# Moving the making of weight forms from GpSimd to VectorE, and reordering two pairs of steps in the tail, in a fused two-layer graph network

## The chip, the cores and the metric

The kernel runs on one NeuronCore of a Trainium2 chip, with all data in float32. The metric is the device time of one execution in microseconds (us), the median of three runs. Engines are named as the profile names them: PE is TensorE (PEld its weight loads), DVE is VectorE, ACT is ScalarE, POOL is GpSimd, and SP is SyncE, which issues most of the DMA transfers.

## The reference

There are 128 graphs of 128 nodes with 256 features, x of shape (128, 128, 256), and a 0/1 adjacency matrix for each. Two layers follow one another. Cut to what matters:

```
# layer 0: attention with 8 heads, values by relation, then a feed-forward part
q, k = x @ Wq + bq, x @ Wk + bk
attn = softmax(q k^T / sqrt(32))
out  = sum over r of (attn * (adj == r)) @ (x @ Wv[r] + bv[r])
x    = norm(x + out @ Wo + bo)
x    = norm(x + gelu(x @ W1 + b1) @ W2 + b2)          # W1 256x1024, W2 1024x256
# layer 1: two graph-attention layers, then a feed-forward part
for W, a in ((W1g, a1), (W2g, a2)):
    h   = h @ W
    att = softmax over axis 1 of where(adj > 0, leaky_relu(h a_l + (h a_r)^T), -9e15)
    h   = att @ h
x = norm(x + h)
x = norm(x + relu(x @ w_ff1 + b_ff1) @ w_ff2 + b_ff2)
```

## The kernel before

The tokens are worked on in 32 groups of four graphs (512 tokens). A group passes through these stages: projections to q, k and v; attention; first feed-forward part (first_ffn); two graph layers (layer1); second feed-forward part (second_ffn). Several groups are in flight at once, each in another stage.

The large products (projections, both feed-forward parts) are done with seven block products in place of eight, a Winograd form of Strassen's scheme. For this each weight is held as four blocks, B11, B21, B22 and one more, and needs four more forms, T1 to T4, that are differences of blocks. The function combined(w), lines 182 to 184, makes them once for each weight, by four subtractions: T3 = B22 - T1 (the slot T1 holds the fourth block at first), T1 = T1 - B11, T2 = B22 - T1, T4 = B21 - T2. For w1, w2, u1 and u2 (the two feed-forward parts' weights) each subtraction covers 128x512 elements, for wqk and wv 128x256. The two groups at the start use the plain blocks of wqk and wv, so T1 of these may only be overwritten when those projections are done (the generator projections; the later one is projected).

The order of the work is written out by hand. Each stage is a Python generator that gives out one unit of work at a time; in_order(...) calls them in the order of its arguments, and a pair (f1, 4) means four units of f1. A callable in the list, such as lambda: combined(w1), is issued at that place. Each engine takes its own instructions strictly in that order; PE, ACT, DVE, SP and POOL all run this way. The names in the lists: pr and pr1 are projections, at and at1 attention, n0, n1_ and so on the steps of a norm, f1 and f2 the units of the two feed-forward parts, gwu the making of the graph layers' weights, l1 the units of layer1, turned the transposition of a group ahead of a feed-forward part.

Lines that the steps below name:

- L184: the four subtractions of combined.
- L725, masked: the exponentials e are multiplied by adj, four times 128x512, to give pm. L754, sums: the products pav of e and pm with v. L771, L773 and L776 divide by the sums.
- L595: the second half of v gets its bias, read from PSUM; L594 is ACT's copy of the first half.
- L334, L335, L344, L349: the norm's variance plus eps (DVE), its power -1/2 (POOL), the shift (DVE), and the scaling of x by ACT. L367: the multiplication and the addition of the norm's rows.
- In ffn, one pass r over half of the hidden columns issues the units in this order: T3 (into the bank called pe, copied to p7 by L456), T2 (into seeded, copied to p16 by L460), B21 (into pa, activated by L435), T1 (into seeded; L466 adds p7, then L435), T4 (into pe; L470 adds p16, then L435), the next pass's B11, and B22 (into seeded; L435, then L479 to L481 make h2 and h3, then L483 seeds the bank again). There are two passes; product2 (L420) follows.
- In layer1: pw (L862) are the products with the graph weights, one for each of the four graphs, evicted by ACT's copies wh (L866). pr (L815) spreads a column, L834 adds it, L838, L840 and L844 to L851 make the attention matrix gs. py (L875) are the products with gs, evicted by ACT's copies yh (L878). The products pg (L888) end the second graph layer. pw and py each use banks of the pool ps_s, of which there are two, so that the third product waits until the first has been evicted.

Only the last group, in the tail after the loop, has layer1 interleaved with the second feed-forward part of the group ahead of it and with nothing else.

Of the kernel before, what the change touches and what calls it, by code (L numbers as in the profile page):

```python
# [107 lines left out]
def fast_pass(ctx, tc, a, out):  # L108
# [5 lines left out]
    nc = tc.nc  # L114
# [22 lines left out]
    def load_xT(g):  # L137

        xt = (w2p if g == 1 else w1p).tile(
            [P, NCH, T], F32, tag="yT" if g == 1 else "xT", name=f"xT_{g}"  # L140
        )
        nc.sync.dma_start(
            xt, xT[:, g * T : (g + 1) * T].rearrange("(c p) t -> p c t", p=P)
        )
        return xt
# [20 lines left out]
    def halved(name, half):  # L166


        kh, nh = half(0).shape[0] // 2, half(0).shape[1]
        w = k.tile([P, 7, kh // P, nh], "w_" + name)  # L170

        for i, j, h in ((B11, 0, 0), (B21, 1, 0), (T1, 0, 1), (B22, 1, 1)):
            nc.sync.dma_start(
                w[:, i], half(h)[j * kh : (j + 1) * kh, :].rearrange("(c p) n -> p c n", p=P)
            )
        return w

    def forms(name):
        nh = a[name].shape[1] // 2
        return halved(name, lambda h: a[name][:, h * nh : (h + 1) * nh])  # L180

    def combined(w):
        for o, p, q in ((T3, B22, T1), (T1, T1, B11), (T2, B22, T1), (T4, B21, T2)):
            nc.gpsimd.tensor_sub(w[:, o], w[:, p], w[:, q])  # L184


    temp = flat(w1p.tile([P, NF, T], F32, tag="hT", name="temp"))
# [10 lines left out]
    first = dict(g=0, direct=0, xt=load_xT(0))  # L198
    wqk = halved("qk", lambda h: a["L0_gnn_W" + "qk"[h]])
# [3 lines left out]
    wv = halved("v", lambda h: a["L0_gnn_Wv"][h])  # L203
# [14 lines left out]
    w1, b1 = forms("L0_gnn_W1"), k.col("L0_gnn_b1")  # L218
# [4 lines left out]
    w2 = forms("L0_gnn_W2")  # L223
# [13 lines left out]
    u1, c1 = forms("L1_gnn_w_ff1"), k.col("L1_gnn_b_ff1")  # L237
    u2 = forms("L1_gnn_w_ff2")
# [55 lines left out]
    def transposed(y, gc, bc, n):  # L294

        yT = w2p.tile([P, NCH, T], F32, tag="yT", name="yT_" + n)
        for c in range(NCH):
            pt = ps_s.tile([P, T], F32, tag="s", name=f"pt_{n}_{c}")
            for b in range(G):
                nc.tensor.transpose(  # L300
                    pt[:, b * P : (b + 1) * P], y[:, b, c * P : (c + 1) * P], k.ident
                )
            nc.scalar.activation(  # L303
                yT[:, c, :], pt, AF.Identity, bias=bc[:, c : c + 1], scale=gc[:, c : c + 1]
            )
        return yT
# [74 lines left out]
    def turned(S, i):  # L381
        n = f"{i}_{S['g']}"
        S["xT", i + 1] = yT = transposed(S["x"], *cols[i], n)
        if i == 1:
            return

        S["yS", i + 1] = ys = w1p.tile([P, 4, TH], F32, tag="yS", name="yS_" + n)
        a11, a21, a12, a22 = (yT[:, c, h * TH : (h + 1) * TH] for c in range(2) for h in range(2))
        nc.vector.tensor_sub(ys[:, 2], a11, a21)
        nc.vector.tensor_add(ys[:, 0], a21, a22)  # L390
        nc.vector.tensor_sub(ys[:, 1], a22, ys[:, 2])
        nc.vector.tensor_sub(ys[:, 3], a12, ys[:, 1])
# [142 lines left out]
    def table(func):  # L535

        nc.scalar.activation(k.none, k.eps[:1], func)

    gelu, exp = lambda: table(AF.Gelu), lambda: table(AF.Exp)
# [384 lines left out]
    with tc.manual_schedule(engines={ET.PE, ET.Activation, ET.DVE, ET.SP, ET.Pool}):  # L924


        for _ in range(4):
            nc.tensor.matmul(seeded, k.ident, over(k.ident), start=True, stop=True)
        none = iter(())
        st = [first, second] + [None] * (NG - 2)  # L930
        S1 = st[1]
        gwu, pr, at = graph_weights(), projections(first), attention(first)
        pr1, at1 = projections(S1), attention(S1)
        n0, n1_, n0_ = norm(first, 0), norm(first, 1), norm(S1, 0)

        def output_bias():
            pb = mm_tile("pb0")
            for c in range(NCH):
                nc.tensor.matmul(
                    pb[:, :D], b0[:, c : c + 1].to_broadcast([P, P]), wo[:, c, :],  # L940
                    start=(c == 0), stop=(c == NCH - 1),
                )
            nc.vector.tensor_add(bo, bo, pb[:, :D])
            prepared(first)

        in_order(
            lambda: combined(w1), (pr, 4), (at, 2), (pr, 2), at, (pr, 2), at, lambda: combined(w2), (at, 3), (pr1, 2),
            at, output_bias, at, (pr1, 2), (at, 3), pr1, at, (at1, 2), n0, n0, pr1, at1, lambda: turned(first, 0), (at1, 2),
        )
        f1 = first_ffn(first)  # L950
        prepared(S1)
        st[2] = entered(2)
        pr = projected(st[2])
        in_order(
            gelu, (f1, 4), pr1, f1, f1, at1, at1, f1, pr1, lambda: combined(wqk), lambda: combined(wv), lambda: combined(u1), f1, n0, at1, (f1, 2), n0, f1, at1,
            (f1, 3), gwu, at1, f1, gwu, f1, at1, gwu,
            f1, at1, f1, gwu, at1, lambda: combined(u2), f1, n0_, pr, n0_, (f1, 4), n1_, (pr, 5), lambda: turned(S1, 0),
        )
        for g in range(NG - 1):
            S, S1 = st[g], st[g + 1]  # L960
            more = g + 2 < NG
            f1, f2 = first_ffn(S1), second_ffn(S)
            n1, n2 = norm(S1, 1), norm(S, 2)
            at = n0 = none
            if more:
                S2 = st[g + 2]
                at, n0 = attention(S2), norm(S2, 0)
            ahead = lambda: turned(S, 2)
            ready = (lambda: prepared(st[g + 2])) if more else (lambda: None)
            if g == 0:  # L970
                l1 = layer1(S)
                in_order(
                    f1, n1_, (pr, 2), (f1, 3), lambda: turned(S, 1), (pr, 2), f1, (n0_, 2), f1, l1, f1, (n1_, 2), l1, l1, f1, l1,
                    (f1, 2), (l1, 2), (pr, 2), f1, l1, (pr, 2), f1, pr, l1, f1, l1, f1, (l1, 2), exp, f1, (at, 2), (l1, 2),
                )
            else:
                n3 = norm(st[g - 1], 3)
                in_order(
                    pr, lambda: turned(S1, 0), (pr, 2), *(() if more else (f2_,)), f1, l1, gelu, (pr, 2), f2_, n3, f1, l1, pr,
                    n0_, f1, (pr, 2), (f1, 3), n0_, l1, f1, (pr, 2), l1, f1, n3, (pr, 2), f1, l1, f1, n3, (pr, 2),  # L980
                    (f1, 3), n3, lambda: store(st[g - 1]), f1, (n1_, 2), exp, (at, 2), f1, (l1, 3),
                )
            in_order(
                f1, (pr, 2), l1, f1, (pr, 2), at, f1, (pr, 2), l1, n2, (pr, 2), f1, n2, (pr, 2), f1, (pr, 2), f1, (pr, 2), *((ahead,) if more else ()), at, f1, n1,
                *(() if more else (ahead,)),
            )
            if not more:
                break
            l1 = layer1(S1)
            pr = none  # L990
            if g + 3 < NG:
                st[g + 3] = entered(g + 3)
                pr = projected(st[g + 3])
            in_order(
                f2, at, (f2, 2), n1, at, f2, at, (f2, 2), lambda: turned(S1, 1), f2, at, (n2, 2), (f2, 2),
                at, f2, l1, ready, (f2, 3), l1, f2, at, f2, l1, (f2, 2), at, at, f2, at, n0, l1, f2,
                n0, l1, pr, f2, *((f2,) if g + 3 < NG else ()),
            )
            n0_, n1_, f2_ = n0, n1, f2
        in_order(f2, n1, (f2, 2), lambda: turned(S1, 1))  # L1000
        l1 = layer1(S1)
        in_order(
            (f2, 2), (l1, 3), f2, l1, (f2, 2), (l1, 2), n1, (f2, 2), l1, n1, (f2, 2), (l1, 2), f2, l1, n2, f2, (l1, 3), n2,
            (f2, 3), l1, (f2, 2), l1,
        )
        n2, n3 = norm(S1, 2), norm(S, 3)
        in_order(n2, f2, n2, (f2, 3), lambda: turned(S1, 2))
        f2 = second_ffn(S1)
        in_order(f2, n3, (f2, 3), n2, n3, (f2, 4), n2, n3, (f2, 4), n3, lambda: store(S), (f2, 2))
        checks()  # L1010
        in_order((f2, 6))
        root(S1, 3, pair(1))
        in_order(f2)
        normed(S1, 3, pair(1))
        in_order(f2)
        root(S1, 3, pair(0))
        for p in (1, 0):
            if p == 0:
                normed(S1, 3, pair(0))
            for step in range(2):  # L1020
                scaled(S1, 3, step, (p,))
            store(S1, pair(p))
# [345 lines left out]
```

## Time and profile before

Time: 2780.09 us, median of 3 runs (2779.88 to 2780.28). The profiled execution has a span of 2778.7 us and a mean granted PE clock of 0.996.

| engine | busy, us | share of the span | instructions |
|---|---|---|---|
| PE | 2725.9 | 98% | 21621 |
| PEld | 2372.0 | 85% | 21621 |
| DVE | 2287.3 | 82% | 5296 |
| ACT | 1613.9 | 58% | 3589 |
| POOL | 166.7 | 6% | 161 |

Matmuls are pipelined, and their ends are modelled, so that a busy PE isn't PE at its peak. Of POOL's 166.7 us, 133.4 us are the 129 powers of L335, spread over the whole run, and 30.9 us the 24 subtractions of L184, all in the first 87 us. In the lines of a group the columns after the bar are the busy time and the mean duration of one in ns, and after the second bar the idle time of the engine just ahead of these instructions, with what ended it. In a timeline a line is: start in us, duration in us, engine, source line, operation, out<-in, shape, count, and in brackets the idle time before and what ended it; several like instructions are merged, so the start of the next line can lie within a merged one.

### The profile page before, as it was taken

Reading aid. Unit: us, or ns where it says so; the run is one execution under the profiler, and the core shown is the slowest. Engines: PE = TensorE matmul, PEld = TensorE weight load, DVE = VectorE, ACT = ScalarE, POOL = GpSimd, SP = SyncE. Lnnn points to the kernel's source line nnn. Section 1 sums busy time; section 2 is a strip of 40 time slices with the busy share of each in tenths; the row PEclk is TensorE's granted clock in tenths of the full one; section 3 lists DMA queues with packets and bytes.
Section 4 is the critical chain, followed back from the end, with each engine's and each line's share of the span. In section 5 each row is a group of like instructions: output and inputs, shape, how many; then the busy total and the mean of one; then the engine's idle time right before and its main releaser. Section 6 shows DMA issues by size and latency. Waiting matters only on the chain.

```text
span 2778.7 us, 54158 instructions
## 1 busy us (share of the span) xinstructions
PE 2725.9 (98%) x21621; PEld 2372.0 (85%) x21621; DVE 2287.3 (82%) x5296; ACT 1613.9 (58%) x3589; POOL 166.7 (6%) x161
## 2 busy tenths in 40 slices
PE   8899999999999999999999999999999999999997
PEld 5688888888888888888888888888888888888876
DVE  5778888888888888888888888888888888888876
ACT  4456556556565566565565565565655665655653
POOL 2200000000000000000000000000000000000000
PEclk9999999999999999999999999999999999999999
DMA  6001100010100101000101000111001110001000
GB/s 177 1 24 32 35 16 28 32 35 32 35 16 24 35 32 35 24 28 24 35 32 35 16 30 29 35 31 35 17 24 35 32 35 27 25 24 35 13 12 17
DMA packets 70234, 86.12 MB, mean 31 GB/s; under 512 B 8428, under 2 KB 48728, under 8 KB 69976
## 3 DMA queue, kind: packets, MB, share of 16 engines
q1 hardware_dynamic: 68872, 82.20, 9.5%
q8 instruction: 172, 2.82, 0.4%
q14 instruction: 86, 0.70, 0.1%
q10 hardware_dynamic: 1104, 0.40, 0.1%
HBM read 65.68 MB, written 16.90 MB: 30 GB/s over the span
## 4 chain that ended last, share of the span: by engine, by line
PE 89%; ACT 4%; DVE 3%; issue 3%; DMA 1%; SPq 0%; ACTq 0%; POOL 0%; DVEq 0%; POOLq 0%
PE po L420 16%; PE ph L411 13%; PE seeded L411 13%; PE seeded L420 12%; PE pqqa L641 4%; PE pwo L789 4%; PE pw L862 4%; PE pvqa L641 4%; PE pav L754 3%; PE pt L300 3%; PE pvqb L641 3%; PE pqqb L641 3%; PE ps L709 2%; PE py L875 2%; PE pg L888 2%
## 5 line engine op out<-in xcount | busy, mean ns | idle before, releaser
L349 ACT ACTIVATE x<-x,sh,rs 128x256 f32<-128x256 f32 x388 | 201.4, 590 | 424.3 <-DVE sh L344 424.3
L335 POOL TENSOR_TENSOR rs<-rs,mhalf 128x4 f32<-128x4 f32 x129 | 133.4, 1034 | 2554.3 <-DVE rs L334 2310.6
L466 DVE TENSOR_TENSOR hT<-seeded,p 128x512 f32<-128x512 f32 x128 | 88.5, 691 | 156.0 <-ACT hT L435 89.5
L411 PE MATMUL seeded<-yS,w_L_gnn_w_ff 128*128 128x256 f32 x768 | 207.3, 392 | 4.9 <-ACT seeded L483 2.2
L411 PE MATMUL seeded<-yS,w_L_gnn_W 128*128 128x256 f32 x768 | 202.0, 386 | 3.2 <-ACT seeded L483 2.2
L411 PE MATMUL ph<-yT,w_L_gnn_w_ff 128*128 128x256 f32 x768 | 200.9, 385 | 0.9 <-ACT yT L303 0.9
L411 PE MATMUL ph<-yT,w_L_gnn_W 128*128 128x256 f32 x768 | 197.4, 379 | 0.4 <-ACT yT L303 0.4
L320 DVE BATCH_NORM_STATS2 st<-x 128x6 f32<-128x256 f32 x512 | 192.1, 417 | 6.7
L411 PEld LDWEIGHTS seeded<-yS,w_L_gnn_w_ff 128*128 128x128 f32 x768 | 138.1, 190 | 63.1 <-ACT seeded L483 28.1
L420 PE MATMUL po<-w_L_gnn_W,hT 128*128 128x128 f32 x1536 | 190.0, 277 | 0.0
L420 PEld LDWEIGHTS po<-w_L_gnn_W,hT 128*128 128x128 f32 x1536 | 183.9, 192 | 6.8
L420 PE MATMUL po<-w_L_gnn_w_ff,hT 128*128 128x128 f32 x1536 | 187.0, 275 | 0.0
L420 PEld LDWEIGHTS po<-w_L_gnn_w_ff,hT 128*128 128x128 f32 x1536 | 184.1, 192 | 3.3
L411 PEld LDWEIGHTS ph<-yT,w_L_gnn_w_ff 128*128 128x128 f32 x768 | 141.1, 190 | 43.3 <-issue 25.2
L411 PEld LDWEIGHTS seeded<-yS,w_L_gnn_W 128*128 128x128 f32 x768 | 138.5, 190 | 40.6 <-DVE hT L466 12.1
L725 DVE TENSOR_TENSOR pm<-e,adj 128x512 f32<-128x512 f32 x256 | 170.2, 725 | 0.0
L411 PEld LDWEIGHTS ph<-yT,w_L_gnn_W 128*128 128x128 f32 x768 | 145.6, 190 | 20.8 <-ACT yT L303 0.7
L435 ACT ACTIVATE hT<-hT,c_L_gnn_b 128x256 f32<-128x256 f32 x256 | 109.5, 497 | 60.2 <-DVE hT L466 58.5
L715 ACT ACTIVATE e<-ps 128x512 f32<-128x512 f32 x256 | 129.8, 589 | 7.5 <-PE ps L709 7.4
L435 ACT ACTIVATE hT<-hT,c_L_gnn_b_ff 128x256 f32<-128x256 f32 x256 | 110.1, 514 | 33.9 <-DVE hT L466 29.6
L834 ACT ACTIVATE gs<-spread,wh 128x128 f32<-128x128 f32 x120 | 38.4, 390 | 156.9 <-DMA spread<-hbm 156.9
L420 PEld LDWEIGHTS seeded<-w_L_gnn_W,hT 128*128 128x128 f32 x1024 | 124.3, 192 | 3.5 <-DVE hT L517 0.2
(196 smaller groups left out, 6522.0 us busy)
## 6 DMA issues: line engine op xcount, KB each, us to landing
xT<-in_xT_dram SPq DMA_DIRECT2D x32, 512.0 KB, 5.8
x<-in_x_dram SPq DMA_DIRECT2D x32, 512.0 KB, 5.1
out_dram<-x SPq DMA_DIRECT2D x31, 512.0 KB, 2.9
spread<-hbm SPq DMA_DIRECT2D x59, 256.0 KB, 3.2
adj<-in_adjT_dram SPq DMA_DIRECT2D x32, 256.0 KB, 4.2
w_L_gnn_W<-in_L_gnn_W_dram SPq DMA_DIRECT2D x8, 256.0 KB, 6.7
w_L_gnn_w_ff<-in_L_gnn_w_ff_dram SPq DMA_DIRECT2D x8, 256.0 KB, 5.0
hbm<-line SPq DMA_DIRECT2D x59, 2.0 KB
```

Source lines behind the costliest of these rows:

```text
L320: nc.vector.bn_stats(st[:, b % 2, :], S["x"][:, b, :])
L335: nc.gpsimd.tensor_tensor(rs[:, bs], rs[:, bs], k.mhalf[:, bs], op=ALU.pow)
L349: nc.scalar.activation(x[:, b, :], x[:, b, :], AF.Identity, bias=sh[:, b : b + 1], scale=rs[:, b : b + 1],)
L411: nc.tensor.matmul(bank[:, s * TH : (s + 1) * TH], wa[:, form, 0, f * P : (f + 1) * P], m, start=start and s == 0, stop=True, skip_group_c ...
L420: nc.tensor.matmul(bank[:, s * P : (s + 1) * P], m[:, f, s * P : (s + 1) * P], wb_[:, form, f, :], start=start and s + f == 0, stop=True, ...
L435: nc.scalar.activation(o[:, s], o[:, s] if src is None else src[:, s * TH : (s + 1) * TH], func, bias=ba[:, f : f + 1],)
L466: nc.vector.tensor_add(hidden(1, 1, r), halves(seeded), halves(p7))
L641: nc.tensor.matmul(bank[:, s * TH : (s + 1) * TH], *ops, start=start and s == 0, stop=True, skip_group_check=True,)
L715: nc.scalar.activation(e[:, s], pss[s], AF.Exp, scale=SCALE)
L725: nc.vector.tensor_mul(pm[:, s], S["e", p][:, s], S["ad"][:, pair(p), None, :].to_broadcast([P, 2, NCH, P]),)
L789: nc.tensor.matmul(po[:, s * D : (s + 1) * D], oT[:, c, b * P : (b + 1) * P], wo[:, c, :], start=(c == 0), stop=(c == NCH - 1),)
L862: nc.tensor.matmul(pw[:, :NU], yT[:, c, b * P : (b + 1) * P], wu[:, c, :], start=(c == 0), stop=(c == NCH - 1),)
```

## The change

GpSimd no longer makes the forms; the same 24 subtractions are issued on VectorE, each moved in the written order to a place meant to meet an idle VectorE: w1 not at the start but after the second step of the first norm; w2 in the first feed-forward part of the first group, after four of its units; wqk and wv somewhat earlier and apart; u1 and u2 at the start of the first turn of the main loop. In the tail, one feed-forward unit (T1 of either pass) is put between the first and the second pair of pw and of py, where before both pairs followed after it.

```
     def combined(w):
         for o, p, q in ((T3, B22, T1), (T1, T1, B11), (T2, B22, T1), (T4, B21, T2)):
-            nc.gpsimd.tensor_sub(w[:, o], w[:, p], w[:, q])
+            nc.vector.tensor_sub(w[:, o], w[:, p], w[:, q])
...
         in_order(
-            lambda: combined(w1), (pr, 4), (at, 2), (pr, 2), at, (pr, 2), at, lambda: combined(w2), (at, 3), (pr1, 2),
-            at, output_bias, at, (pr1, 2), (at, 3), pr1, at, (at1, 2), n0, n0, pr1, at1, lambda: turned(first, 0), (at1, 2),
+            (pr, 4), (at, 2), (pr, 2), at, (pr, 2), (at, 4), (pr1, 2),
+            at, output_bias, at, (pr1, 2), (at, 3), pr1, at, (at1, 2), n0, n0, lambda: combined(w1), pr1, at1, lambda: turned(first, 0), (at1, 2),
         )
...
         in_order(
-            gelu, (f1, 4), pr1, f1, f1, at1, at1, f1, pr1, lambda: combined(wqk), lambda: combined(wv), lambda: combined(u1), f1, n0, at1, (f1, 2), n0, f1, at1,
+            gelu, (f1, 4), lambda: combined(w2), pr1, f1, f1, at1, at1, f1, lambda: combined(wqk), pr1, lambda: combined(wv), f1, n0, at1, (f1, 2), n0, f1, at1,
             (f1, 3), gwu, at1, f1, gwu, f1, at1, gwu,
-            f1, at1, f1, gwu, at1, lambda: combined(u2), f1, n0_, pr, n0_, (f1, 4), n1_, (pr, 5), lambda: turned(S1, 0),
+            f1, at1, f1, gwu, at1, f1, n0_, pr, n0_, (f1, 4), n1_, (pr, 5), lambda: turned(S1, 0),
         )
...
             if g == 0:
                 l1 = layer1(S)
                 in_order(
-                    f1, n1_, (pr, 2), (f1, 3), lambda: turned(S, 1), (pr, 2), f1, (n0_, 2), f1, l1, f1, (n1_, 2), l1, l1, f1, l1,
+                    f1, n1_, lambda: combined(u1), lambda: combined(u2), (pr, 2), (f1, 3), lambda: turned(S, 1), (pr, 2), f1, (n0_, 2), f1, l1, f1, (n1_, 2), l1, l1, f1, l1,
...
         in_order(f2, n1, (f2, 2), lambda: turned(S1, 1))
         l1 = layer1(S1)
         in_order(
-            (f2, 2), (l1, 3), f2, l1, (f2, 2), (l1, 2), n1, (f2, 2), l1, n1, (f2, 2), (l1, 2), f2, l1, n2, f2, (l1, 3), n2,
+            f2, l1, f2, (l1, 2), f2, l1, (f2, 2), (l1, 2), n1, (f2, 2), l1, n1, f2, l1, f2, l1, f2, l1, n2, f2, (l1, 3), n2,
             (f2, 3), l1, (f2, 2), l1,
         )
```

## The prediction

> **What bounds the kernel now.** I read the page's share of each engine first: PE is busy for 98% of the span, so a change can only win where PE is held up. The 40 slices show that this is at the two ends (8 in the first slice, 7 in the last, 9 between). So I then read the waits of PE in the first 160 us, the busy times by stretch, and the timeline of both ends.
>
> The largest wait of PE there (columns: total us, times, longest), and the stretch 78 to 93 us (busy us of PE, PEld, DVE, ACT and POOL, the granted clock, the DMA):
> ```profile
> PE pav L754 <- DVE pm L725: 7.8, 8, 3.3
> 78.00:93.00 15.00, 8.90 (x70) 6.10 (x71) 11.61 (x9) 2.13 (x7) 8.77 (x6) 0.66 0.00 0
> ```
> PE waits for VectorE's masking (pm), at 0.66 of its clock, while GpSimd works. The timeline of that place, and the same masking in a later group:
> ```profile
> 73.66 13.43 POOL L184 TENSOR_TENSOR w_L_gnn_w_ff<-w_L_gnn_w_ff 128x512 f32<-128x512 f32 x8
> 75.84 3.43 DVE L367 TENSOR_TENSOR x<-x,r_L_gnn_g 128x512 f32<-128x512 f32 x2
> 79.19 6.76 DVE L725 TENSOR_TENSOR pm<-e,adj 128x512 f32<-128x512 f32 x4
> 89.13 1.85 PE L411 MATMUL seeded<-yS,w_L_gnn_W 128*128 128x256 f32 x4
> ...
> 2625.10 2.48 DVE L725 TENSOR_TENSOR pm<-e,adj 128x512 f32<-128x512 f32 x4
> ```
> Four masks take 6.76 us beside GpSimd and 2.48 us alone; four 128x256 products take 1.85 us there against 1.03 elsewhere. GpSimd's work that the change removes (mean ns of one ahead of the bar's end):
> ```profile
> L184 POOL TENSOR_TENSOR w_L_gnn_w_ff<-w_L_gnn_w_ff 128x512 f32<-128x512 f32 x8 | 13.0, 1624 | 0.5
> L184 POOL TENSOR_TENSOR w_L_gnn_W<-w_L_gnn_W 128x512 f32<-128x512 f32 x8 | 11.8, 1476 | 22.2 <-DMA w_L_gnn_W<-in_L_gnn_W_dram 21.7
> L184 POOL TENSOR_TENSOR w_v<-w_v 128x256 f32<-128x256 f32 x4 | 3.2, 807 | 16.8 <-PE pv L590 16.6
> L184 POOL TENSOR_TENSOR w_qk<-w_qk 128x256 f32<-128x256 f32 x4 | 2.9, 726 | 0.2
> ```
>
> [...]only such instructions stretch (L725, L367, L479 to L481), from about 0.6 us to 1.1 to 1.75 us each; reciprocals beside heavy DMA keep their 1.7 us, and two L555 adds at 37.3 us, with the DMA engines full and GpSimd idle, take their usual 1.29 us. [...]a pair of one GpSimd and one VectorE instruction takes 1.67 us here, about what GpSimd's takes. [...]here 1.48 to 1.62 us against 0.69. [...]Here PE has nearly nothing from 77.7 us, and the matmuls are at half speed from 81 us on.
>
> **The change, part one: the head.** Prices from the trace: independent 128x512 adds on VectorE start every 0.605 us (L367), dependent ones every 0.71 us (L479 to L480); for 128x256 it is 0.34 and 0.46 us (L389 to L392). In the built program each of a weight's last three subtractions waits for the one before it, so one combined() costs 3x0.71 + 0.61 = 2.74 us, or 3x0.46 + 0.34 = 1.72 us for wqk and wv. In all 4x2.74 + 2x1.72 = 14.4 us of new VectorE work. Where it goes are four idle times of VectorE (in brackets, what ended them):
> ```profile
> 53.70 0.42 DVE L595 TENSOR_TENSOR v<-pv,bv 128x256 f32<-128x256 f32 x1 [2.40 <-ACT v L594]
> 64.41 0.42 DVE L595 TENSOR_TENSOR v<-pv,bv 128x256 f32<-128x256 f32 x1 [2.79 <-ACT v L594]
> 71.76 0.42 DVE L595 TENSOR_TENSOR v<-pv,bv 128x256 f32<-128x256 f32 x1 [3.07 <-ACT v L594]
> 124.93 0.69 DVE L466 TENSOR_TENSOR hT<-seeded,p 128x512 f32<-128x512 f32 x1 [5.36 <-PE seeded L411]
> ```
> w1 goes ahead of the first (2.40 us, and 0.5 more because L344, 0.68 us beside GpSimd, is 0.15 alone), w2 ahead of the second, wqk ahead of the third, u1 and u2 ahead of the fourth. 2.74 in 2.9, 2.74 in 2.79 and 1.72 in 3.07 cost nothing; 5.48 in 5.36 costs 0.1 us. Only wv, behind the third L595, has work queued behind it that PE waits for (L479 to L481, L367, pm): 1.72 us on the path. All these weights have long landed, as GpSimd read w1 at 18.6 and w2 at 30.1 us.
>
> What is won, along the path:
> 1. First attention: from the first pav product to the next scores 3.70 us (24.27 to 27.97), for what takes 1.77 us undisturbed (2614.60 to 2616.37). 1.9 us.
> 2. Second attention: from the first pav to the next projection 2.58 us (36.16 to 38.74) against 1.77. 0.8 us, together 2.7; a further 0.1 at the third. The second xT, issued at 17.0 us and landing in at most 7.3 us, doesn't hold this up.
> 3. From VectorE's L479 (72.10) to the end of the four masks (85.95): 13.85 us. Without GpSimd: 1.72 for wv, 0.71 + 2x0.61 for L479 to L481, 2x0.605 for L367, 3x0.605 + 0.69 for the masks, 7.36 us. 6.5 us, together 9.3.
> 4. The clock, if it stays up: the remaining pav products take 1.72 us instead of 3.13 (86.00 to 89.13), and those from 89.13 to 91.83 take 1.77 instead of 2.70. 2.3 us.
> Sum: 2.8 + 6.5 + 2.3 - 0.1 = 11.5 us. From 92 us on the order is unchanged and each engine follows the others, so I carry it to the end undiminished. The loads for the third group are issued at 42 to 45 us and don't come into it.
>
> **Part two: the tail.** The two moved pairs of rows on PE (py_0, py_1 and pw_0, pw_1) go ahead of a unit called T1 here, whose product goes into seeded. Now:
> ```profile
> 2712.48 0.69 DVE L851 TENSOR_TENSOR gs<-gs,gr 128x512 f32<-128x512 f32 x1
> 2713.23 1.14 PE L875 MATMUL py<-wh,gs 128*128 128x258 f32 x4 [0.44 <-DVE gs L851]
> 2714.29 0.68 DVE L466 TENSOR_TENSOR hT<-seeded,p 128x512 f32<-128x512 f32 x1
> 2715.01 0.91 ACT L435 ACTIVATE hT<-hT,c_L_gnn_b_ff 128x256 f32<-128x256 f32 x2 [2.41 <-DVE hT L466]
> 2715.82 0.62 ACT L878 COPY yh<-py 128x258 f32<-128x258 f32 x2
> 2716.22 1.14 PE L875 MATMUL py<-wh,gs 128*128 128x258 f32 x4 [1.86 <-ACT yh L878]
> ```
> The copy of py_0 stands behind T1's activation, that behind L466, that behind L367 (2713.09), and PE behind the copy, for a bank. In the new order T1's product (0.87 us) no longer fills the wait for L851, so PE is idle about 1.6 us ahead of py_0; but then py_0/1, T1, py_2/3 follow without a gap. From the end of unit B21 to the start of T4: now 2711.56 to 2717.20, 5.64 us; then 1.66 + 3x0.87 = 4.27 us. 1.4 us. For pw the second half of yT isn't evicted before 2699.50, so pw_0 can't use all of its earlier place: the last pw ends at 2703.43 for 2703.6, and pr 0.3 us sooner. Together 1.7 us; what follows (pr, gs, pg, the norms) is one chain and moves along.
>
> 2780.1 - 11.5 - 1.7 = **2766.9 us**.
>
> **The rivals.** (a) PE loses its clock even so: it has sparse work from 74.9 to 76.6 us (new times), and after a gap of 1.81 us in the tail (2736.42) products at 2739 us ran at 1.85 us. Then the 2.3 us stay: 2769.2. Against: the gap is shorter than that of before, and dense work comes just ahead. (b) The tail's swap gives nothing, as PE idles for L851 in place of the bank: 2768.6. Against: the sum above; for: such reckoning of a few tenths over four engines is loose. (c) The gain of the head is swallowed later, by something that doesn't move along, a load or a wait I have not seen: 2780.1 - 1.7 to 2780.1 - 6, about 2776. Against: PE at 98% with small waits. (d) Slower: the 14.4 us of subtractions all come to lie on VectorE's path, as the slots are tight, and what is won is only the 7.8 us that PE is seen waiting for pm: 2780.1 + 14.4 - 7.8 = 2786.7. Against: the four idle times are measured, and as long as what goes in, to 0.1 us.
>
> **Chances.** Forecast 0.72, (a) 0.12, (b) 0.08, (c) 0.04, (d) 0.04. The forecast's own looseness is about 1.5 us either way (a combined() between 4x0.605 and 4x0.71, the pipelining of PE); with (a) and (b) inside, the range is 2764.5 to 2770.5. Faster by over 0.2% (5.6 us) are the first three: 0.92; (c) 0.04 the same; (d) 0.04 slower.
>
> **What would show it.** In the new profile: no L184 on POOL; L184 on DVE at 0.69 and about 0.4 us; L725 at 0.69 us everywhere; the unit now at 91.83 us begun near 80.3; PEclk at 1.00 in 70 to 90 us; L466 (now 124.93) idle about zero before; py_2 without a wait and py_0 with one of about 1.6 us. I am wrong if L725 stays long without GpSimd, if L595 now waits behind L184, or if the start of the main loop moves by over 2 us less than the head's sum.

## The result, and the profile after

| | before | after |
|---|---|---|
| median of 4 runs each, us | 2779.99 (2779.53 to 2780.28) | 2769.52 (2769.24 to 2769.79) |
| span of the profiled execution, us | 2778.7 | 2767.9 |
| mean granted clock of PE | 0.996 | 0.998 |
| POOL busy, us (instructions) | 166.7 (161) | 136.0 (137) |

The ratio of the times is 0.9962, 95% interval 0.9945 to 0.998. The change makes the kernel 10.5 us faster; 13.2 us had been forecast, and 2769.5 us lies within the range that was given.

The stretch from 78 to 93 us, in the columns of the prediction (busy us of PE, PEld, DVE, ACT and POOL, the granted clock, the DMA):

```profile
78.00:93.00 15.00, 15.00 (x146) 13.80 (x138) 11.84 (x29) 3.43 (x9) 0.00 (x0) 1.00 0.00 1
```

and PE's wait for the masks in the list of waits of the first 160 us:

```profile
PE pav L754 <- DVE pm L725: 0.8, 4, 0.2
```

In this stretch PE is busy throughout at full clock, where it was busy for 8.90 us at 0.66 of it, and of 7.8 us of waiting 0.8 are left. VectorE's timeline shows where the subtractions L184 went (start, duration, and in brackets the idle time before):

```profile
49.26 2.87 DVE L184 TENSOR_TENSOR w_L_gnn_W<-w_L_gnn_W 128x512 f32<-128x512 f32 x4
52.20 0.42 DVE L595 TENSOR_TENSOR v<-pv,bv 128x256 f32<-128x256 f32 x1
...
70.04 0.42 DVE L595 TENSOR_TENSOR v<-pv,bv 128x256 f32<-128x256 f32 x1 [1.36 <-ACT v L594]
70.38 1.79 DVE L184 TENSOR_TENSOR w_v<-w_v 128x256 f32<-128x256 f32 x4
...
75.22 2.49 DVE L725 TENSOR_TENSOR pm<-e,adj 128x512 f32<-128x512 f32 x4
...
109.05 5.64 DVE L184 TENSOR_TENSOR w_L_gnn_w_ff<-w_L_gnn_w_ff 128x512 f32<-128x512 f32 x8
114.61 0.69 DVE L466 TENSOR_TENSOR hT<-seeded,p 128x512 f32<-128x512 f32 x1
```

The first of the three L595 now follows w1's forms without idle time, u1 and u2 fill the place ahead of L466 (begun at 124.93 us before), and the last four masks of the second group take 2.49 us for 6.76.

The tail on PE, where py had waited 0.44 and 1.86 us. First the two pr (L815) of the kernel before, which had no wait ahead of them:

```profile
2703.67 1.12 PE L815 MATMUL pr<-ident,wh 128*128 128x128 f32 x8
...
2718.06 1.05 PE L815 MATMUL pr<-ident,yh 128*128 128x128 f32 x8
```

and the changed kernel, with two lines of ScalarE:

```profile
2693.71 1.16 PE L815 MATMUL pr<-ident,wh 128*128 128x128 f32 x8 [0.30 <-ACT wh L866]
...
2703.30 1.14 PE L875 MATMUL py<-wh,gs 128*128 128x258 f32 x4 [1.50 <-DVE gs L851]
2704.28 1.03 PE L411 MATMUL seeded<-yS,w_L_gnn_w_ff 128*128 128x256 f32 x4
2705.14 1.03 PE L875 MATMUL py<-wh,gs 128*128 128x258 f32 x4
...
2706.14 0.91 ACT L435 ACTIVATE hT<-hT,c_L_gnn_b_ff 128x256 f32<-128x256 f32 x2 [1.29 <-DVE hT L466]
2706.95 0.62 ACT L878 COPY yh<-py 128x258 f32<-128x258 f32 x2
2707.35 1.16 PE L815 MATMUL pr<-ident,yh 128*128 128x128 f32 x8 [0.32 <-ACT yh L878]
```

py behaves as forecast: 1.50 us ahead of the first pair and nothing ahead of the second. But pr, the next in the chain, now waits 0.30 and 0.32 us for ScalarE's copies, which stand behind the activation L435 and with it behind VectorE's L466.

For the comparison of all runs two stretches serve, both between events on PE. The **head** goes from the first projection pq to the first pgt (L264, behind the second group's attention), the **tail** from the last po (L420) ahead of the last group's feed-forward work to the first pt (L300) of the last norm.

| kernel | first pq | head, us | tail, us | median time, us |
|---|---|---|---|---|
| before | 6.83 | 89.54 | 49.24 | 2779.99 |
| after | 7.87 | 78.07 | 48.91 | 2769.52 |
| after again (e5) | 7.68 | 78.07 | 48.91 | 2770.44 |
| head alone (e1) | 7.70 | 78.07 | 50.83 | 2771.62 |
| head alone again (e12) | 7.15 | 79.78 | 49.23 | 2771.59 |
| head alone, PE filled (e6) | 7.93 | 78.07 | 49.79 | 2770.66 |
| tail alone (e2) | 7.58 | 87.92 | 48.91 | 2779.12 |
| wv later (e3) | 6.52 | 77.63 | 48.91 | 2767.87 |
| swap of py alone (e4) | 6.61 | 78.07 | 48.47 | 2769.26 |
| GpSimd reads beside it (e7) | 6.63 | 86.76 | 48.93 | 2779.79 |
| GpSimd only writes (e8) | 7.74 | 78.07 | 48.93 | 2769.92 |
| last copies on VectorE (e9) | 7.11 | 79.77 | 47.96 | 2769.09 |
| all three improvements (e10) | 6.41 | 77.61 | 47.46 | 2766.26 |
| before, PE filled (e11) | 7.69 | 87.26 | 49.24 | 2778.32 |

In the first comparison the times of each kernel lay within 0.8 us; in the later ones those of one kernel spread over up to 5.2 us, which goes with the clock (last section). These later times were taken in three groups, each with its own runs of the kernel before: 2781.93 us beside e1 to e4, 2780.88 beside e5 to e8, 2780.68 beside e9 to e12. Small differences are therefore read from the two stretches. Between them, from pgt to po, the fourteen profiles lie within 0.3 us of each other; behind the tail they differ by up to 1.6 us (41.69 to 43.27), again with the clock.

### The profile page after: what moved, and what is told of

Same layout as the page of the kernel before. It is cut to its first block, busy times and chain, and to the rows that moved or that the text cites. A ratio compares the mean times of both kernels' runs of the same rounds, so it can differ in the third digit from the quotient of the medians.

```text
span 2767.9 us, 54145 instructions
## 1 busy us (share of the span) xinstructions
PE 2722.6 (98%) x21621; PEld 2369.9 (86%) x21621; DVE 2285.9 (83%) x5320; ACT 1613.8 (58%) x3589; POOL 136.0 (5%) x137
## 4 chain that ended last, share of the span: by engine, by line
PE 90%; ACT 4%; issue 3%; DVE 3%; POOL 0%; ACTq 0%; POOLq 0%; DVEq 0%
PE po L420 16%; PE ph L411 13%; PE seeded L411 13%; PE seeded L420 12%; PE pwo L789 4%; PE pw L862 4%; PE pqqa L641 4%; PE pvqa L641 4%; PE pav L754 3%; PE pt L300 3%; PE pvqb L641 3%; PE pqqb L641 3%; PE ps L709 3%; PE py L875 2%; PE pg L888 2%
## 5 line engine op out<-in xcount | busy, mean ns | idle before, releaser
L466 DVE TENSOR_TENSOR hT<-seeded,p 128x512 f32<-128x512 f32 x128 | 88.5, 692 | 151.4 <-ACT hT L435 88.4
L420 PE MATMUL po<-w_L_gnn_W,hT 128*128 128x128 f32 x1536 | 190.0, 277 | 0.0
L420 PEld LDWEIGHTS po<-w_L_gnn_W,hT 128*128 128x128 f32 x1536 | 183.9, 192 | 6.8
L420 PE MATMUL po<-w_L_gnn_w_ff,hT 128*128 128x128 f32 x1536 | 187.0, 275 | 0.0
L420 PEld LDWEIGHTS po<-w_L_gnn_w_ff,hT 128*128 128x128 f32 x1536 | 184.1, 192 | 3.2
L725 DVE TENSOR_TENSOR pm<-e,adj 128x512 f32<-128x512 f32 x256 | 159.1, 683 | 0.0
L435 ACT ACTIVATE hT<-hT,c_L_gnn_b 128x256 f32<-128x256 f32 x256 | 109.5, 498 | 51.3 <-DVE hT L466 49.5
L435 ACT ACTIVATE hT<-hT,c_L_gnn_b_ff 128x256 f32<-128x256 f32 x256 | 110.1, 514 | 32.8 <-DVE hT L466 29.1
L420 PEld LDWEIGHTS seeded<-w_L_gnn_W,hT 128*128 128x128 f32 x1024 | 124.3, 192 | 3.5 <-DVE hT L517 0.3
```

Of the source, the lines that this page charges most:

```text
L420: nc.tensor.matmul(bank[:, s * P : (s + 1) * P], m[:, f, s * P : (s + 1) * P], wb_[:, form, f, :], start=start and s + f == 0, stop=True, ...
L435: nc.scalar.activation(o[:, s], o[:, s] if src is None else src[:, s * TH : (s + 1) * TH], func, bias=ba[:, f : f + 1],)
L466: nc.vector.tensor_add(hidden(1, 1, r), halves(seeded), halves(p7))
L725: nc.vector.tensor_mul(pm[:, s], S["e", p][:, s], S["ad"][:, pair(p), None, :].to_broadcast([P, 2, NCH, P]),)
```

## The experiments

**Theory**: GpSimd's reads of SBUF held up VectorE's instructions with two SBUF inputs (four masks took 6.76 us beside GpSimd and 2.48 alone), and the wait for these cost PE its clock as well (0.66 from 78 to 93 us); in the tail the swap shortens one wait, but pr inherits another. **Rivals**: the order of the work, or the time at which the forms are ready, is what counts; and the tail is worth its 1.7 us, so that the head gave less than reckoned.

**e1 and e12, the head alone.** The last group's list is that of before:

```
-            f2, l1, f2, (l1, 2), f2, l1, (f2, 2), (l1, 2), n1, (f2, 2), l1, n1, f2, l1, f2, l1, f2, l1, n2, ...
+            (f2, 2), (l1, 3), f2, l1, (f2, 2), (l1, 2), n1, (f2, 2), l1, n1, (f2, 2), (l1, 2), f2, l1, n2, ...
```

> Part one alone: the weights' forms on VectorE, the last group's order as before. Theory 1 (the tail's swaps gave nothing, as the spreads pr wait in their turn for copies that stand behind T1's activation on ScalarE): 2769.8 us, within 0.5 us of the changed kernel; in the tail pw, pr and py stand as in the kernel before, 10.2 to 10.4 us earlier. Rival (the tail gives the 1.7 us of the prediction, and the head 1.2 us less than reckoned): 2771.2 us, that is 1.7 us above the changed kernel.

> Part one alone once more, for a second look at the old order of the tail beside the two versions of the new one. Theory 1 (the old order loses its clock behind the wait of 1.86 us, in some executions only): from the last po to the first pt either 49.2 us (clock kept) or 50.8 us (lost), the mean of the times 0.3 to 1.9 us above the changed kernel. Rival (the drop seen in the first look was a single event): 49.2 us, and 0.3 us above.

The head took the same 78.07 us in e1 as in the changed kernel. The times, 2771.6 us twice, are near the rival's 2771.2, and the traces show why neither side had it right. PE's timeline of e1, in the tail:

```profile
2705.85 1.14 PE L875 MATMUL py<-wh,gs 128*128 128x258 f32 x4 [1.86 <-ACT yh L878]
...
2708.39 1.92 PE L815 MATMUL pr<-ident,yh 128*128 128x128 f32 x8
```

Behind the wait of 1.86 us, pr takes 1.92 us, where it took 1.05 in the kernel before: PE has fallen to half clock, and the tail is 1.59 us longer than in the kernel before, with the same instructions in the same order. In e12 the tail kept its clock (49.23 us), but the head lost it, in a projection that takes 3.70 us elsewhere:

```profile
29.27 5.40 PE L579 MATMUL pq<-xT,w_qk 128*128 128x512 f32 x8 [1.64 <-ACT e L715]
```

**e2, the tail alone**: the forms on GpSimd as before, with the new list in the tail.

> Part two alone: the last group's order changed, the weights' forms still on GpSimd. Theory 1: 2779.7 us, at most 0.5 us below the kernel before: T4 begins 1.3 us earlier (2715.9 for 2717.2), but pr behind pw ends 0.4 us later and pr behind py gives 0.6 us back. Rival (the tail's swaps give what was reckoned): 2778.3 us.

The tail took 48.91 us for 49.24: 0.33 us by its order, the same as in the changed kernel. The times were lower than that allows, 2779.12 us for 2781.93 beside it (ratio 0.9994, interval 0.9986 to 1.0002); the means of 13 and 17 runs differ by 1.8 us, with two standard errors of 1.1 us. That is the difference the rival had, 1.7 us, though by the traces the order does not give it. The new tail kept its clock between po and pt in all nine profiles that have it or a variant of it; the old one lost it in one of four (before, e1, e11, e12), which at 1.59 us would add 0.4 us on average, not 1.5. The mean clock recorded for each run narrows the rest down. It was 0.995 in nine of the 17 runs of the kernel before (mean 2782.8 us) and in five of e2's 13 (2781.1), and 0.997 in two of the one (2779.1) and in seven of the other (2778.5). At 0.997 the two kernels are 0.6 us apart; much of the 1.8 us goes with the clock, which e2 kept more often. Where the other runs lost theirs, in the tail or elsewhere, this does not show, so that this part stays open.

**e6, filling PE's gap in the old tail.**

```
         for b in range(G):
+            if b == 2 and S["g"] == NG - 1:
+                fill = ps_1.tile([P, T], F32, tag="qa", name="fill")
+                for _ in range(12):
+                    nc.tensor.matmul(fill[:, :P], k.ident, k.ident, start=True, stop=True)
             py = ps_s.tile([P, T], F32, tag="s", name=f"py_{n}_{b}")
```

> Part one alone (tail in the order of before), with 12 additional products of ident by ident into the free bank qa between py_1 and py_2, where PE is idle for 1.86 us; their result is not used. Theory 1 (on this path the old order's real cost is the clock, which falls to half after that idle time in some executions: pr after py 1.92 us for 1.05): pr takes 1.05 us, from the last po to the first pt 49.2 us, the whole within 0.5 us of the changed kernel. Rival (the order itself is worth 1.8 us): the fill gains nothing, 1.8 us above the changed kernel, 50.8 us from po to pt.

pr took 1.05 us, and the tail 49.79 us: not the 49.24 expected, since each product ran as two instructions and the fill lasted 2.84 us, longer than the gap, but a full microsecond less than in e1. Work of no use to anybody made the kernel no slower: 2770.66 us for the 2771.6 of e1 and e12 (ratios to the kernels before beside them 0.9962, 0.9966 and 0.9965). The mean clock was 0.998 in four of e6's five runs, and 0.997 in ten of the eleven of e1 and e12. That goes with the clock, and against an order worth 1.8 us by itself. The intervals of the three ratios overlap, and only one profile has the gap unfilled and the clock lost.

**e5, the changed kernel again**, beside e6 to e8.

> The changed kernel again, for the same chip as the next three. Theory 1 (the start of PE's first products lies up to 1.3 us apart between executions by the phase of its clock; the tail's new order costs no clock): from PE's last po of the loop's end (2676.83 in the first profile) to the first pt of the last norm (2725.74) 48.9 us again, and about 2769.5 us. Rival (the new tail loses its clock in some executions as the old one does): 50 us or more there.

Head and tail came out to the hundredth as in the first profile.

**e7 and e8, GpSimd put back beside VectorE.** GpSimd works through as many elements as it did (in 40 operations 256 wide for 24), but into a scratch tile (16-bit) that nobody reads; in e7 it reads two parts of a weight, in e8 it only fills the tile. In e8 the two lines under c are `nc.gpsimd.memset(idle, 0.5)`. The calls for the other four weights, not shown here, stand where the kernel before made their forms.

```
+    def shadow(w):
+        for o in range(4):
+            for c in range(w.shape[2] * w.shape[3] // D):
+                p, q = (w[:, b].rearrange("p c n -> p (c n)")[:, c * D : (c + 1) * D] for b in (B22, B21))
+                nc.gpsimd.tensor_sub(idle, p, q)
...
+            lambda: shadow(w1), (pr, 4), (at, 2), (pr, 2), at, (pr, 2), at, lambda: shadow(w2), (at, 3), (pr1, 2),
```

> The changed kernel, and GpSimd beside it subtracts parts of weights (128x256 f32, two inputs in SBUF) into a small scratch at the places where it made the forms before; nobody reads the scratch. Theory 1 (VectorE's instructions with two SBUF inputs are held up by GpSimd's reads): L725 again 1.6 us each beside GpSimd, PE again at half clock around 85 us, the whole 2777 to 2784 us (more than before is possible, as VectorE now makes wv's forms there too). Rival (what counted was when the forms are ready and where they stood in the order): 2769.5 us, as the changed kernel's forms are where they were.

> As the run before, but GpSimd fills the scratch with a constant (128x256, no input from SBUF), as often. Theory 1 [...]: L725 stays at 0.69 us, 2769.5 us, within 1 us of the changed kernel. Rival (any work of GpSimd on SBUF, or its load on semaphores and queues, slows VectorE): 2774 us or more.

Timelines of e7, POOL first (its lines are numbered 8 higher from L189 on, so that L733 is L725 and L603 is L595):

```profile
57.48 15.94 POOL L193 TENSOR_TENSOR idle<-w_L_gnn_w_ff 128x256 bf16<-128x256 f32 x16
...
49.33 4.09 DVE L184 TENSOR_TENSOR w_L_gnn_W<-w_L_gnn_W 128x512 f32<-128x512 f32 x4
53.33 0.41 DVE L603 TENSOR_TENSOR v<-pv,bv 128x256 f32<-128x256 f32 x1
53.67 4.28 DVE L733 TENSOR_TENSOR pm<-e,adj 128x512 f32<-128x512 f32 x4
...
65.82 4.60 DVE L184 TENSOR_TENSOR w_L_gnn_W<-w_L_gnn_W 128x512 f32<-128x512 f32 x4
```

All of e7's two-input instructions from 49 to 70 us are stretched (2.87 to 4.09 and 4.60, 2.49 to 4.28), while L603, which reads one input from PSUM, keeps its 0.41. The kernel is almost as slow as before (2779.79 us for 2780.88 beside it), though the forms are made where the change puts them and GpSimd's work is wanted by nobody. The expectation missed the size (1.07 us for each of the stretched masks, not 1.6) and the place: as nothing holds this work back, its second part ran from 48.7 to 73.4 us, and the second group's last four masks, later, kept their 2.49 us at full clock. The delay arose ahead of them: at the first group's masks (4.42 and 4.07 us for four), at the forms of w1 and w2, at the second group's first four masks (4.28), and in 6.83 us of half clock from 52.7 us on. The third L595 began 70.86 us behind the first pq for 62.17 in the changed kernel, which is all of the head's 8.69 us. In e8 (its lines are numbered 7 higher) the same places, beside GpSimd's fills:

```profile
48.97 8.79 POOL L192 MEMSET idle<- 128x256 bf16 x24
...
49.13 2.87 DVE L184 TENSOR_TENSOR w_L_gnn_W<-w_L_gnn_W 128x512 f32<-128x512 f32 x4
52.08 0.42 DVE L602 TENSOR_TENSOR v<-pv,bv 128x256 f32<-128x256 f32 x1
52.42 2.49 DVE L732 TENSOR_TENSOR pm<-e,adj 128x512 f32<-128x512 f32 x4
```

None of these is stretched, the head takes 78.07 us, and the time is within 0.6 us of that of e5. So here GpSimd's reads count (4.28 us for four masks in e7) and its fills, which only write, do not (2.49 us in e8), and the rival of order and readiness falls. A fill takes 0.31 us where a subtraction took 0.9, so that GpSimd was busy for a shorter time; but its fills lay beside VectorE's work for all of these lines of e8.

**e11, the clock by itself.** The kernel before, with products into a free bank while PE waits for the masks of the second group.

```
+                        if S["g"] == 1 and p == 1 and u + c == 0 and r == 1:
+                            for _ in range(3 if s == 0 else 1):
+                                nc.tensor.matmul(fill, k.ident, over(k.ident), start=True, stop=True)
```

> The kernel before with extra products of ident into the free bank qa where PE waits for the masks of the second group (three of 512 columns ahead of the first, one ahead of each of the next three); their result is not used. Theory 1 (the half clock behind that wait is a cost of its own, beside the masks): the products of pav after the fourth mask take 1.7 us for 2.8 to 3.1, the next three units 2.8 us for 2.9 to 3.7, the whole 1.2 to 2.3 us below the kernel before. Rival (the clock there is hidden or falls anyway): no change.

With GpSimd still in the way, the stretch of 78 to 93 us now reads, in the columns as above:

```profile
78.00:93.00 15.00, 13.88 (x107) 7.88 (x100) 13.23 (x12) 3.94 (x11) 9.55 (x6) 1.00 0.00 1
```

The clock holds, and the head takes 87.26 us: 2.28 us less than in the profile before, of which 0.11 lie ahead of the third L595 and so ahead of the filled wait. It is only 0.66 less than in e2's profile, whose clock fell for 6.83 us and not 10.24, and whose third L595 came 0.6 us sooner than e11's. The medians are 2778.32 and 2780.68 us (ratio 0.9991, interval 0.9983 to 1.0), and the mean clock was 0.998 in twelve of e11's 13 runs, but 0.995 to 0.997 in all 17 of the kernel before. The clock is a cost of its own beside the masks.

**e3, wv's forms later.**

```
-            ... lambda: combined(wqk), pr1, lambda: combined(wv), f1, n0, at1, ...
+            ... lambda: combined(wqk), pr1, f1, n0, at1, ...
...
-                    ... (n1_, 2), l1, l1, f1, l1,
+                    ... (n1_, 2), l1, l1, f1, lambda: combined(wv), l1,
```

> The changed kernel with wv's forms not between L595 and L479 of the second group but after u1 and u2, in the first turn of the main loop, just ahead of L838 (VectorE idle 3.3 us there). Theory 1 (VectorE's queue from L595 over L479, L367 and the masks is the path of the head, so its 1.79 us of wv are paid in full): the masks L725 end 1.8 us earlier and the whole is 1.5 to 1.8 us faster than the changed kernel, 2767.9 us. Rival (PE or ScalarE ends last there once GpSimd no longer reads): masks earlier, but PE's following unit not, 2769.5 us, no change.

The median is 2767.87 us, as theory 1 had it. From L595 to the end of the masks VectorE needs 5.97 us for 7.68 in e4, and PE follows: from the second unit ahead of pden to the first behind the masks 4.89 us for 6.60. Both differ by 1.71 us, so wv was on the path in full. The head as a whole shows 0.44 us of it, since in this execution PE lost 1.3 us to its clock at 52 us, ahead of the moved work. The agreement of the median with 2767.9 is therefore partly luck.

**e4, the swap of py alone**: pw's rows in the old order.

> The changed kernel with only the swap of py kept; the rows of pw in the order of before. Theory 1 (the swap of pw costs 0.4 us, that of py gains 0.7 net): 2769.1 us, 0.4 us below the changed kernel; pr behind pw starts without a wait, pr behind py still waits 0.3 us for the copy of yh. Rival (the swaps of pw and py each gain, 0.3 and 1.4 us): 0.3 us above the changed kernel, 2769.8 us.

The tail takes 48.47 us, 0.44 less than with both swaps. So the swap of py gains 0.77 us, and that of pw loses 0.44. The times (2769.26 us) can't tell this from the changed kernel's.

**e9, the copies behind which pr waits moved off ScalarE.**

```
-            nc.scalar.copy(wh[:, b, :], pw[:, :NU])
+            (nc.vector.tensor_copy if S["g"] == NG - 1 and b > 1 else nc.scalar.copy)(wh[:, b, :], pw[:, :NU])
...
-            nc.scalar.copy(yh[:, b, :], py[:, : D + 2])
+            (nc.vector.tensor_copy if S["g"] == NG - 1 and b > 1 else nc.scalar.copy)(yh[:, b, :], py[:, : D + 2])
```

> The changed kernel, but in the last group the copies of the third and fourth pw and py go to VectorE instead of ScalarE, where they stand behind T1's activation. Theory 1 (pr's wait of 0.30 and 0.32 us after the changed kernel's swaps is for these copies, held up in ScalarE's order): pr begins without a wait, from the last po to the first pt 48.2 to 48.4 us for 48.91, the whole 0.5 to 0.7 us below the changed kernel. Rival (pr waits for the last copy's data anyway, wherever it is made): 48.9 us, no change.

PE's timeline of e9:

```profile
2707.33 1.05 PE L815 MATMUL pr<-ident,yh 128*128 128x128 f32 x8
```

pr begins behind the unit ahead of it, without a wait, and the tail takes 47.96 us for 48.91. That is 0.95 us, more than the two waits of 0.30 and 0.32: each pr also begins about 0.16 us ahead of the recorded end of the products in front of it, which the waiting ones did not. What held pr was the order on ScalarE, where these copies stood behind T1's activation and so behind L466. Of the time, 2769.09 us, little can be read: the profiled execution lost its clock for 3.41 us at 29 us, and at 2726 us, behind the tail, for 6.83 us, where the other profiles lose it for 3.41.

**e10, what the experiments point to**: wv later, pw's rows in the old order with all their copies on VectorE, py's swap with its last two copies there.

> The changed kernel with wv's forms moved to the first turn of the main loop, the rows of pw in the order of before with their copies on VectorE, the swap of py kept with its last two copies on VectorE. Theory 1: 1.8 us less in the head, 1.1 us in the tail (po to pt 47.8 us), together 2.9 us below the changed kernel, about 2767 us. Rival (the copies on VectorE delay its adds L466 and L470, on which PE's next units wait): the tail gains 0.4 us alone, 2768 us.

2766.26 us, ratio to before 0.9953 (0.9939 to 0.9967), against 0.9961 (0.9947 to 0.9974) for the changed kernel in e5. The tail takes 47.46 us, 1.45 us less. The medians differ by 4.2 us and the means (2767.6 and 2770.2) by 2.6, near the 2.9 expected. It is the fastest kernel of the study; the intervals overlap, so that this rests on the stretches.

## Why the prediction was right, and where not

**The head came out as reckoned.** Up to the first pgt the two profiles differ by 11.47 us, for 2.8 + 6.5 + 2.3 = 11.6; the slot of u1 and u2 lies behind it. Step by step:

| step | forecast, us | measured, us |
|---|---|---|
| first to third attention, start of the third L595 less the start of pq (64.93, then 62.17) | 2.8 | 2.76 |
| VectorE from L479, or from wv's forms, to the end of the masks (13.85, then 7.33) | 6.5 | 6.52 |
| from there to the unit of 91.83 us, now 81.40 (5.88, then 3.69) | 2.3 | 2.19 |
| u1 and u2 in the slot ahead of L466, its start less that of the first pgt (28.56, then 28.66) | -0.1 | -0.1 |

w1 and w2 took up the idle time ahead of L595 and cost nothing that this sum shows. The split is confirmed by runs and not only by reading: e11 alone gives 2.28 us, nearly all of it the clock's, and the rest, 87.26 - 78.07 = 9.19 us, is what the prediction had as 2.8 + 6.5. That the first step agrees to 0.04 us is partly luck: in the two other profiles with the forms on GpSimd, e11's and e2's, the third L595 comes 64.82 and 64.23 us behind pq, and the step would be 2.65 or 2.06 us. The instructions that stretched beside GpSimd in the profile before (L725, L367, L479 to L481, to between 1.0 and 1.8 us each) all read two inputs from SBUF. That GpSimd's reads are the cause is shown by e7 and e8: four masks took 4.28 us beside its subtractions and 2.49 us beside its fills.

**The step that failed is the tail's sum.** "1.4 us" for py and "0.3 us" for pw were followed by "what follows (pr, gs, pg, the norms) is one chain and moves along". T4 did begin earlier, by 1.27 us net of what came before, but 0.59 of this was lost at the very next instruction: pr needs the copies of the third and fourth py, for its data and for a bank of ps_s, and in the new order these copies stand on ScalarE behind T1's activation. The prediction had seen this queue ahead of py_2 and forgot it behind. For pw the same wait of 0.30 us, with a pw_0 that waits for the second half of yT (2.25 us for 1.92), turned a gain of 0.3 into a loss of 0.44 (e4). In all the tail gave 0.33 us of 1.7. Rival (b), a tail that gives nothing, was the nearest case, but not for the reason it gave: the wait for L851 was in the sum and came out shorter than reckoned (1.50 us for 1.6).

The remaining microsecond is no step of the change. The first pq began 1.04 us later in the profile after than in that before (7.87 for 6.83), and everything behind it. The same eight products stand ahead of it; they took 5.63 us before and 6.66 after. They begin every 0.86 us at first, at half clock, and every 0.43 us once the clock has risen, which it does at 5.28 us before and at 7.36 after. At half clock half of the time is lost, and half of the 2.08 us between the two is 1.04. The other profiles go the same way: over all fourteen the clock rises between 4.43 us (e10) and 7.49 us (e6), and pq begins at 6.41 and 7.93 us there. Two profiles of one kernel (e1 and e12) differ by 0.5 us in it, so that the change has no part in this, and how it fell in the two profiles compared is chance. So the span's 10.8 us are 11.47 of the head, less 1.04 of the start and 0.08 of the main loop (with the slot of u1 and u2), and 0.33 more in the tail and 0.10 at the end.

**Rival (a)**, that PE loses its clock even so, was right as a possibility and wrong of its place: behind the masks it held in every profile with the change, but at 29 us (e9, e12) or 52 us (e3, e10) it was lost, at a cost of 1.2 to 1.7 us, in four of the ten profiles with the forms on VectorE and no reads of GpSimd beside them. Rivals (c) and (d) fell: nothing was swallowed in the main loop, and the slots held. One reading was off without harm: the page gives PE 8 tenths in its second slice too, not 9.

## What to carry to other kernels

Before work is given to GpSimd because it is idle, look at what VectorE does beside it: here VectorE's instructions with two SBUF inputs were stretched by GpSimd's reads (four masks took 6.76 us for 2.48), and PE, which bounds the kernel, waited 7.8 us for the masks. Moving 24 subtractions, 30.9 us of GpSimd's time, won 11.5 us of the head. On VectorE those that got a measured idle slot cost nothing or 0.1 us, and those that got none, wv's, cost 1.71 us in full. When two steps are swapped, follow the queue of every engine that touches them to the next consumer, not only to the step that is swapped: the copy that no longer holds up the next product may hold up the one behind it. And a wait of PE can have a second price, its clock (here behind waits of 1.64 and 1.86 us, in some executions), so shortening or filling such waits can pay where the order alone would not.

## What the runs showed of the hardware

The half clock comes in pieces of one length. By the traces' record of the clock it lasted 3.41 us in e1's tail, 3.41 at 52 us in e3, 3.41 at 29 us in e12, 6.83 in e2's head (two pieces) and 10.24 in that of the kernel before (three). In all fourteen traces each later change of the clock comes a whole number of 3.413 us after its first rise, as 2720.42 us, or 797 pieces, in the changed kernel. The first rise itself comes at no fixed time, but 4.43 to 7.49 us behind the first instruction.

What I had not expected is how little it takes. In the kernel before PE was busy for 0.77 us of the 3.41 us ahead of the drop at 80.38 us, and against rival (a) the prediction set that its gap is shorter. The later runs show drops behind less idle time. In the 3.41 us ahead of the drops of e1, e9 and e12 PE was busy for 1.55 to 1.77 us, with a single wait of 1.64 us at 29 us or 1.86 us in the tail; ahead of those at 52 us in e3 and e10 it was busy for 2.2 to 2.3 us, with no wait above 0.69. Whether the clock was lost went with when the execution began: at 29 us it was lost in the profiles whose first pq began at 7.11 and 7.15 us and not in those from 7.68 on; at 52 us in those at 6.41 and 6.52, and not in that at 6.61 (e7 aside, which has longer waits there). Behind the wait of 1.81 us ahead of the last norm's first pt, which is followed by shorter ones, it was lost in all fourteen. What decides it is not shown: the wait of 1.86 us lay within a single piece of 3.413 us in e1 and in e12, and only e1 lost its clock.

One kernel's times are several microseconds apart with this. Of the 17 runs of the kernel before beside e1 to e4, the nine with a mean clock of 0.995 took 2782.8 us on average, and the two at 0.997 took 2779.1; e10's five lie between 2766.0 and 2769.9 us.
